# A feed-forward kernel on one core: each of the seven half-size products of the last block's first product formed from seven smaller ones

## The chip, the cores and the metric

One core of a Trainium2 chip. Times are device microseconds of one execution, from three runs of the kernel before; the profile is of one further execution. TensorE multiplies matrices into PSUM banks, VectorE (DVE in the profile) and ScalarE (ACT) read PSUM and SBUF, GpSimd (POOL) works on SBUF, and SyncE (SP) issues most of the DMAs.

## The reference

x is 64 batches of 64 rows of 512 features, all fp32. The conditioning part makes a row vector q per batch, mixes each row with the batch's sum, and multiplies by a 512 x 512 matrix; the second part multiplies by another 512 x 512 matrix and adds low-rank expert terms with a router:

```
q_emb = relu(cond @ W3 + b3)                      # one row of 512 for each batch
v     = (n * x + sum over rows of x) * q_emb      # 64 x 64 x 512
y     = relu(v @ W2 + b2)                         # the first wide product
gates = softmax(y @ W_router + b_router); the best 2 of 6 kept
out   = x + y @ W_base + b_base + (y @ A_s) @ B_s + sum over experts of ((y @ A_r) * gate) @ B_r
```

## The kernel before

Features lie on the 128 partitions, four chunks c of 128 features, and rows lie along the free dimension. The 4096 rows are worked in four blocks k of 1024; a block has two halves h of 512 rows. Every block does the same four stages on TensorE, one after the other: the first product (y from v and W2), the router and low-rank products (tile ph, line 573, 32 matmuls with y as the stationary operand), the second product (out from y and W_base), and in its midst the transposes of the gated low-rank values (tile pt) and their product with B.

Both wide products of a block are done in the seven-product form of a 2 x 2 block product. The weights are cut into b11 to b22 (256 x 256 each), the rows' features and halves into a11 to a22; weight_sums and row_sums make four sums of each (t and s, lines 133 and 241), VectorE does them with one instruction each. With P1 = a11 b11, P2 = a12 b21, P3 = s3 b22, P4 = a22 t3, P5 = s0 t0, P6 = s1 t1, P7 = s2 t2 the quarters of the result are P1 + P2, U + P5 + P3, U + P7 + P4 and U + P5 + P7, where U = P1 + P6. In the code a product is a call of product (line 147): two fp32 matmuls of 128 x 128 by 128 x 512 for one half j of a result quarter, so 14 calls and 28 matmuls for a block's first product.

first_seven (line 348) does the first product of blocks 1 to 3. For each j it opens four PSUM banks (px, py, pw, pz) of the six in pool ps_p, adds P2, P3 and P4 straight into the banks of P1, P5 and P7 (start=False), has VectorE add U and the banks in temporaries u, u22, u21, u12, and has ScalarE apply bias and relu into y. Pool tmp holds these temporaries, two buffers of 512 columns for each name; the second product uses the same names. first_mixed is block 0, where a half of the rows is done without the seven-product form and the other in it, with 256 columns a matmul.

While TensorE works on block k, the other engines get v and its row sums ready for block k + 1. prepare(k + 1) puts these steps into a list, behind: 17 steps of modulate (a sum on VectorE, 4 batches on ScalarE each) and the four row sums. fill(n) takes n of them and emits them at that place of the engines' queues: 6 for each j in first_seven, and in the second product nine times an equal share of what is left. A block's second product (second, line 417) opens eight results in the six banks, and its VectorE steps are: the gate (from ph), add_u, hw, add_r, and finish for each result, which adds the bias, and sends the result out through SyncE's queue. The tile pool's program order is the order of emission: each engine runs its queue in that order and waits for the others by semaphore.

x has three buffers for four blocks, v has two, and y, s and sy (the row sums of y) one each. ph is formed for half h and column group s in the order (0,0) (0,1) (1,0) (1,1) (0,2) (0,3) (1,2) (1,3), with c innermost.

Of the kernel before, what the change touches and what calls it, by code (L numbers as in the profile page):

```python
# [15 lines left out]
P = 128  # L16
# [18 lines left out]
def adaln_ffn(ctx: ExitStack, tc: tile.TileContext, xa, x0, x1, head, w3, w2, wb, a, bcat, br, outT):  # L35
# [11 lines left out]
    xpool = ctx.enter_context(tc.tile_pool(name="x", bufs=3))  # L47
    vpool = ctx.enter_context(tc.tile_pool(name="v", bufs=2))
    mid = ctx.enter_context(tc.tile_pool(name="mid", bufs=1))
    tmp = ctx.enter_context(tc.tile_pool(name="tmp", bufs=2))  # L50
    tmp1 = ctx.enter_context(tc.tile_pool(name="tmp1", bufs=1))
    small = ctx.enter_context(tc.tile_pool(name="small", bufs=1))
    ps_p = ctx.enter_context(tc.tile_pool(name="ps_p", bufs=6, space=PSUM))
# [80 lines left out]
    def weight_sums(w, name):  # L134

        b11, b12 = w[:, :KH, :DH], w[:, :KH, DH:]
        b21, b22 = w[:, KH:, :DH], w[:, KH:, DH:]
        t = [const.tile([P, KH, DH], F32, tag=f"{name}_{i}", name=f"{name}_{i}") for i in range(4)]
        steps = [
            lambda: nc.vector.tensor_tensor(t[0], b12, b11, ALU.subtract),  # L140
            lambda: nc.vector.tensor_tensor(t[1], b22, t[0], ALU.subtract),
            lambda: nc.vector.tensor_tensor(t[2], b22, b12, ALU.subtract),
            lambda: nc.vector.tensor_tensor(t[3], b21, t[1], ALU.subtract),
        ]
        return {1: b11, 2: b21, 3: b22, 4: t[3], 5: t[0], 6: t[1], 7: t[2]}, steps

    def product(ps, i, j, w, s, start=True):
        for c in range(KH):
# [92 lines left out]
    def row_sums(a, name, cols=slice(0, TB)):  # L241

        a11, a12, a21, a22 = a[:, :KH, 0, cols], a[:, KH:, 0, cols], a[:, :KH, 1, cols], a[:, KH:, 1, cols]
        s = [mid.tile([P, KH, TB], F32, tag=f"{name}{i}", name=f"{name}{i}")[:, :, cols] for i in range(4)]
        steps = [
            lambda: nc.vector.tensor_tensor(s[0], a21, a22, ALU.add),
            lambda: nc.vector.tensor_tensor(s[1], s[0], a11, ALU.subtract),
            lambda: nc.vector.tensor_tensor(s[2], a11, a21, ALU.subtract),
            lambda: nc.vector.tensor_tensor(s[3], a12, s[1], ALU.subtract),
        ]  # L250
        return {1: a11, 2: a12, 3: s[3], 4: a22, 5: s[0], 6: s[1], 7: s[2]}, steps

    behind = []

# [4 lines left out]
    def prepare(k):  # L259
        behind.extend(modulate(k))  # L260
        ss[k], steps = row_sums(vs[k], "s")
        behind.extend(steps)

    def relu(y, f, h, src, cols=slice(0, TB)):
        nc.scalar.activation(y[:, f, h, cols], src, AF.Relu, bias=b2_sb[:, f : f + 1])  # L265

    def first_mixed(y):

        vs[0] = v = vpool.tile([P, NC, 2, TB], F32, tag="v", name="v_0")
        vsum = small.tile([P, NC, BB], F32, tag="vsum", name="vsum_0")
        nq = small.tile([P, NC, BB], F32, tag="nq", name="nq_0")
        half, cols = BB // 2, BB // 2 * NH
        other = slice(cols, TB)
        s, s_steps = row_sums(v, "s", other)

        def part(p, c, f, lo, hi):
            nc.tensor.matmul(  # L279
                p[:, :, lo * NH : hi * NH], w2_sb[:, c, ts(f, P)], v[:, c, :, lo * NH : hi * NH],  # L280
                start=(c == 0 and lo == 0), stop=(c == NC - 1), skip_group_check=True,
            )

        def without_sums(c):
            for j in range(KH):
                nc.tensor.matmul(
                    px[j], w2_sb[:, c, ts(j, P)], v[:, c, 0, other], start=(c == 0), stop=(c % KH == KH - 1),
                    skip_group_check=True,
                )
            if c == KH - 1:  # L290
                for j in range(KH):
                    nc.scalar.copy(p1[j], px[j])

        idle(8)
        embed([0], "pq0")
        idle(2)
        p0 = [ps_p.tile([P, 2, cols], F32, tag="pp", name=f"py_{f}") for f in range(NC)]
        px = [ps_p.tile([P, cols], F32, tag="pp", name=f"yx_0_{j}") for j in range(KH)]
        p1 = [mid.tile([P, cols], F32, tag=f"p1_{j}", name=f"p1_0_{j}") for j in range(KH)]
        for c in range(NC):  # L300
            pieces = ((0, half // 2), (half // 2, half)) if c == 0 else ((0, half),)
            for lo, hi in pieces:
                modulate_group(v, vsum, c, lo, hi)
                for f in range(NC):
                    part(p0[f], c, f, lo, hi)
                if c == 0 and lo == 0:
                    embed(range(1, NC), "pq")
            if c > 0:
                modulate_scalar(v, vsum, nq, c - 1, half, BB)
            if c == NC - 1:  # L310
                modulate_scalar(v, vsum, nq, c, half, BB)
            if c > 1:
                without_sums(c - 2)
        for f in range(NC):
            nc.scalar.activation(y[:, f, :, :cols], p0[f], AF.Relu, bias=b2_sb[:, f : f + 1])
        for c in range(NC - 2, NC):
            without_sums(c)
        for step in t2_steps + s_steps:
            step()
        behind.extend(tb_steps)  # L320
        prepare(1)
        fill(1)
        for j in range(KH):
            relu(y, j, 0, px[j], other)
        for j in range(KH):
            f1, f2 = j, KH + j
            bank = lambda n: ps_p.tile([P, cols], F32, tag="pp", name=f"y{n}_0_{j}")
            temp = lambda n: tmp.tile([P, TB], F32, tag=n, name=f"{n}_0_{j}")[:, :cols]
            py, pw, pz = bank("y"), bank("w"), bank("z")
            u, r, r1, r2 = temp("u"), temp("u22"), temp("u21"), temp("u12")  # L330
            product(py, 6, j, t2, s)
            nc.vector.tensor_tensor(u, py, p1[j], ALU.add)
            product(pw, 5, j, t2, s)
            nc.vector.tensor_tensor(r, pw, u, ALU.add)
            product(pz, 7, j, t2, s)
            nc.vector.tensor_tensor(r, pz, r, ALU.add)
            relu(y, f2, 1, r, other)
            fill(1)
            product(pw, 3, j, t2, s, start=False)
            nc.vector.tensor_tensor(r2, pw, u, ALU.add)  # L340
            relu(y, f2, 0, r2, other)
            fill(1)
            product(pz, 4, j, t2, s, start=False)
            nc.vector.tensor_tensor(r1, pz, u, ALU.add)
            relu(y, f1, 1, r1, other)
            fill(1)

    def first_seven(k, y):

        s = ss[k]  # L350
        if k + 1 < NB:
            prepare(k + 1)
        for j in range(KH):
            f1, f2 = j, KH + j
            bank = lambda n: ps_p.tile([P, TB], F32, tag="pp", name=f"y{n}_{k}_{j}")
            temp = lambda n, pool=tmp: pool.tile([P, TB], F32, tag=n, name=f"{n}_{k}_{j}")
            px, py, pw, pz = bank("x"), bank("y"), bank("w"), bank("z")
            p1, u, r, r1, r2 = temp("p1", tmp1), temp("u"), temp("u22"), temp("u21"), temp("u12")
            product(px, 1, j, t2, s)
            nc.scalar.copy(p1, px)  # L360
            product(py, 6, j, t2, s)
            nc.vector.tensor_tensor(u, py, p1, ALU.add)
            fill(1)
            product(pw, 5, j, t2, s)
            nc.vector.tensor_tensor(r, pw, u, ALU.add)
            fill(1)
            product(pz, 7, j, t2, s)
            nc.vector.tensor_tensor(r, pz, r, ALU.add)  # L368
            relu(y, f2, 1, r)
            fill(2)  # L370
            product(px, 2, j, t2, s, start=False)
            relu(y, f1, 0, px)
            product(pw, 3, j, t2, s, start=False)
            nc.vector.tensor_tensor(r2, pw, u, ALU.add)
            relu(y, f2, 0, r2)
            fill(1)
            product(pz, 4, j, t2, s, start=False)
            nc.vector.tensor_tensor(r1, pz, u, ALU.add)
            relu(y, f1, 1, r1)
            fill(1)  # L380

    w = const.tile([P, 2 * NS, G], F32, tag="w", name="w")
    nc.gpsimd.memset(w[:, :, 0:1], 1.0)
# [33 lines left out]
    def second(k, y, ph):  # L417
# [6 lines left out]
                ps[name, j] = ps_p.tile([P, TB], F32, tag="pp", name=f"o{name}_{k}_{j}")  # L424
            product(ps[name, j], i, j, tb, sy, start=start)

        def temp(n, j, pool=tmp):
            return pool.tile([P, TB], F32, tag=n, name=f"o{n}_{k}_{j}")

        def copy_p1(j):  # L430
            p1s[j] = temp("p1", j, tmp1)
            nc.scalar.copy(p1s[j], ps["x", j])  # L432

        def add_u(j):
# [120 lines left out]
            last_routed(p, cols, hwd)  # L555
            leave(p, cols, 0, us12[1], queue)

    sys_ = {}
    t2, t2_steps = weight_sums(w2_sb, "t2")
    tb, tb_steps = weight_sums(wb_sb, "tb")  # L560
    for k in range(NB):
        y = mid.tile([P, NC, 2, TB], F32, tag="y", name=f"y_{k}")
        if k == 0:
            first_mixed(y)
        else:
            first_seven(k, y)


        ph = ps_h.tile([P, 2 * NS, P], F32, tag="ph", name=f"ph_{k}")

        for h, s in ((0, 0), (0, 1), (1, 0), (1, 1), (0, 2), (0, 3), (1, 2), (1, 3)):
            for c in range(NC):
                nc.tensor.matmul(  # L573
                    ph[:, h * NS + s, :HC], y[:, c, h, ts(s, P)], a_sb[:, c, :],
# [60 lines left out]
```

## Time and profile before

| | us |
|---|---|
| three runs: median (lowest to highest) | 267.84 (267.76 to 268.4) |
| the profiled execution: its time | 268.01 |
| its span, first to last instruction | 266.2 |
| last block: first product, by the chain of waits | 199.90 to 223.93 |
| last block: router products ph | 223.93 to 231.07 |
| last block: second product, to the last VectorE step | 231.07 to 263.3 |

The profile has a page of groups of instructions by line, engine and shape with their count, total and mean time; a chain of waits, followed back from the last instruction; and a timeline with, in brackets, how long an engine sat idle before an instruction and on whom it waited. An fp32 matmul appears as two MATMUL records and two weight loads (engine PEld). In the timeline a record's end is about 0.17 us behind the start of the next record, since matmuls are pipelined: four records of 512 columns are shown with 1.88 us and follow those before at a distance of 1.72. The chain gives the distances.

### The profile page before, as it was taken

The page shows a single profiled execution, that of the slowest core. Times are in us where ns is not written, and L with a number is a line of the kernel's source. Part 1 is how long each engine was busy: PE and PEld are TensorE (multiplying, and loading weights), DVE is VectorE, ACT ScalarE, POOL GpSimd, SP SyncE. Part 2 cuts the span into 40 slices and gives each one's busy share as a digit, 9 for nine tenths or more (in the row PEclk, how much of TensorE's full clock was granted, in tenths as well). Part 3 has the DMA queues.
Part 4 walks back from the last instruction along what each step waited for, and adds up shares of the span by engine and source line. Part 5 has one row for each costly group of instructions (what it writes and reads, how often), then busy time and mean ns, then how long its engine had stood idle before and what let it go on. Part 6 is the DMA issues. An engine that isn't in the chain of part 4 may idle for free.

```text
span 266.2 us, 2629 instructions
## 1 busy us (share of the span) xinstructions
PE 261.3 (98%) x878; PEld 141.6 (53%) x878; DVE 146.6 (55%) x251; ACT 112.8 (42%) x294; POOL 35.7 (13%) x41
## 2 busy tenths in 40 slices
PE   8999999999999999999999999999999999999995
PEld 4746895454444468454444448544444446845542
DVE  2896789646655448623746466823673333762422
ACT  2399389593028991254004996345000314001000
POOL 1000000570000000534000000057000000053400
PEclk9999999999999999999999999999999999999999
DMA  6999200004371000003230000000431000000323
GB/s 187 377 340 409 113 0 0 2 0 158 118 273 81 0 2 0 1 0 118 83 118 0 0 0 0 2 0 0 158 118 40 0 0 2 0 0 0 121 87 113
DMA packets 10303, 20.13 MB, mean 76 GB/s; under 512 B 1216, under 2 KB 3008, under 8 KB 10288
## 3 DMA queue, kind: packets, MB, share of 16 engines
q1 hardware_dynamic: 10000, 19.82, 20.7%
q10 hardware_dynamic: 288, 0.13, 0.2%
q8 instruction: 7, 0.11, 0.2%
q14 instruction: 8, 0.07, 0.1%
HBM read 11.56 MB, written 8.39 MB: 75 GB/s over the span
## 4 chain that ended last, share of the span: by engine, by line
PE 84%; ACT 7%; DVE 4%; DMA 2%; SPq 1%; issue 0%; DVEq 0%
PE oz L149 10%; PE ox L149 10%; PE ph L573 9%; PE ow L149 9%; PE yw L149 8%; PE yz L149 8%; PE yx L149 6%; PE oy L149 5%; PE ow L446 5%; PE yy L149 5%; ACT v L188 3%; PE ox L446 3%; PE oz L446 3%; DMA x<-in_x_dram 2%; ACT v L236 2%; ACT y L265 2%
## 5 line engine op out<-in xcount | busy, mean ns | idle before, releaser
L188 ACT ACTIVATE v<-x,vsum,nq 128x64 f32<-128x64 f32 x192 | 66.4, 429 | 6.7 <-DVE vsum L184 6.7
L440 POOL TENSOR_TENSOR ou<-ou,x 128x512 f32<-128x512 f32 x24 | 29.7, 1266 | 212.6 <-DVE ou L436 212.6
L573 PEld LDWEIGHTS ph<-a_sb,y 128*128 128x128 f32 x256 | 29.4, 192 | 2.2 <-issue 1.4
L573 PE MATMUL ph<-a_sb,y 128*128 128x118 f32 x256 | 29.7, 276 | 0.3 <-ACT y L265 0.3
L149 PE MATMUL ox<-y,wb_sb 128*128 128x512 f32 x64 | 29.5, 593 | 0.0
L265 ACT ACTIVATE y<-u,head_sb 128x512 f32<-128x512 f32 (+1 forms) x24 | 15.9, 664 | 25.0 <-DVE u L368 13.7
L149 PE MATMUL yx<-v,w_sb 128*128 128x512 f32 x48 | 22.6, 592 | 0.0
L360 ACT COPY p<-yx 128x512 f32<-128x512 f32 x6 | 3.5, 579 | 43.1 <-PE yx L149 43.1
L149 PEld LDWEIGHTS ox<-y,wb_sb 128*128 128x128 f32 x64 | 11.8, 190 | 12.9 <-issue 12.9
L452 DVE SCALAR_TENSOR_TENSOR ou<-ow,head_sb,ou 128x512 f32<-128x512 f32 x14 | 10.5, 751 | 11.9 <-PE ow L446 11.4
L436 DVE TENSOR_TENSOR ou<-oy,op 128x512 f32<-128x512 f32 x8 | 5.5, 687 | 17.9 <-PE oy L149 17.9
L149 PEld LDWEIGHTS yx<-v,w_sb 128*128 128x128 f32 x48 | 9.1, 190 | 11.5 <-issue 11.5
L149 PE MATMUL oz<-y,tb 128*128 128x512 f32 x32 | 15.1, 595 | 0.0
L149 PE MATMUL oz<-sy,tb 128*128 128x512 f32 x32 | 15.0, 592 | 0.0
L149 PE MATMUL oy<-sy,tb 128*128 128x512 f32 x32 | 15.0, 592 | 0.0
L279 PE MATMUL py<-v,w_sb 128*128 128x512 f32 (+1 forms) x40 | 14.4, 511 | 0.3 <-DVE v L228 0.3
L183 DVE TENSOR_REDUCE vsum<-x 128x16 f32<-128x1024 f32 x12 | 14.6, 1212 | 0.0
L432 ACT COPY op<-ox 128x512 f32<-128x512 f32 x8 | 4.7, 583 | 21.3 <-PE ox L149 21.3
L452 DVE SCALAR_TENSOR_TENSOR x<-ox,head_sb,x 128x512 f32<-128x512 f32 x8 | 6.0, 751 | 13.7 <-PE ox L446 13.7
L149 PE MATMUL yw<-s,w_sb 128*128 128x512 f32 (+1 forms) x32 | 13.4, 541 | 0.0
L149 PE MATMUL yy<-s,t 128*128 128x512 f32 (+1 forms) x32 | 13.3, 539 | 0.0
L149 PE MATMUL yw<-s,t 128*128 128x512 f32 (+1 forms) x32 | 13.3, 539 | 0.0
(109 smaller groups left out, 348.2 us busy)
## 6 DMA issues: line engine op xcount, KB each, us to landing
x<-in_x_dram SPq DMA_DIRECT2D x12, 512.0 KB, 7.3
out_dram<-ou SPq DMA_DIRECT2D x22, 256.0 KB, 2.0
out_dram<-x SPq DMA_DIRECT2D x8, 256.0 KB, 2.1
x<-in_x_dram SPq DMA_DIRECT2D x7, 256.0 KB, 5.7
w_sb<-in_w_dram SPq DMA_DIRECT2D x4, 256.0 KB, 5.6
wb_sb<-in_wb_dram SPq DMA_DIRECT2D x4, 256.0 KB, 4.9
w_sb<-in_w_dram SPq DMA_DIRECT2D x1, 384.0 KB, 4.6
out_dram<-ou SPq DMA_DIRECT2D x2, 192.0 KB, 1.9
```

Source lines behind the costliest of these rows:

```text
L149: nc.tensor.matmul(ps, w[i][:, c, ts(j, P)], s[i][:, c, :], start=start and c == 0, stop=c == KH - 1, skip_group_check=True,)
L183: nc.vector.tensor_reduce(vsum[:, c, :], xc, AX.XY, ALU.add)
L188: nc.scalar.activation(v[:, c, :, ts(b, NH)], xs[k][:, c, :, ts(b, NH)], AF.Identity, bias=vsum[:, c, b : b + 1], scale=nq[:, c, b : b + 1],)
L236: nc.scalar.activation(v[:, c, :, ts(b, NH)], batches_of(c, b, b + 1)[:, :, 0], AF.Identity, bias=vsum[:, c, b : b + 1], scale=nq[:, c, b ...
L265: nc.scalar.activation(y[:, f, h, cols], src, AF.Relu, bias=b2_sb[:, f : f + 1])
L279: nc.tensor.matmul(p[:, :, lo * NH : hi * NH], w2_sb[:, c, ts(f, P)], v[:, c, :, lo * NH : hi * NH], start=(c == 0 and lo == 0), stop=(c = ...
L432: nc.scalar.copy(p1s[j], ps["x", j])
L436: nc.vector.tensor_tensor(us[j], ps["y", j], p1s[j], ALU.add)
L440: nc.gpsimd.tensor_tensor(split(t[j], x.shape[1]), split(us[j], x.shape[1]), x, ALU.add)
L446: nc.tensor.matmul(ps[name, j], bcat_sb[:, ts(f, P)], hw, start=False, stop=True, skip_group_check=True)
L452: nc.vector.scalar_tensor_tensor(add, split(p, g), bb_sb[:, f : f + 1], add, ALU.add, ALU.add)
L573: nc.tensor.matmul(ph[:, h * NS + s, :HC], y[:, c, h, ts(s, P)], a_sb[:, c, :], start=(c == 0), stop=(c == NC - 1),)
```

## The change

In the last block (k = 3) the first product's seven products are each formed from seven smaller ones. A product of a (256 features x 512 rows) with b (256 x 256) is cut once more: 128 features, 256 rows and 128 outputs. One inner product q(n, t) is then one fp32 matmul of 128 x 128 by 128 x 256. All terms stay, in fp32.

- prepare_inner makes the inner sums. Weight side: four sums for each of the seven outer products, in 12 VectorE instructions (four on 4 x 128 columns, four on 2 x 128, four on 128), in a buffer of pool x; they are attached to steps 2 to 13 of the list behind, in block 2. Row side: four for outer product 1 (256 columns each), four for products 5, 6, 7 and 3 together (1024 columns), at the end of the list, and four for products 2 and 4 (512 columns), emitted in first_inner after the first four matmuls, in the buffer of sy. For this t and s become slices of one tile each.
- first_inner does the last block's first product. Each inner round t has two banks: a holds P1 and P5 in its left and right 256 columns, b holds U and U + P7. ScalarE copies P1 from a to the left of b (seed_y), where TensorE adds P6; it copies that to the right of b (seed_z), where TensorE adds P7 and later P4. P2 and P3 are added in a. VectorE takes the four quarters out with an add to what the outer form needs (ScalarE with a copy in the first two rounds, where there is nothing to add). The rounds overlap: round t's first two matmuls stand before the last ones of rounds t - 1 and t - 2. The outer sums U + P5 and U + P7 + P5 are four GpSimd adds, and the relus into y follow.
- The router products of the last block are formed in the order h = 0, then h = 1; rest(), with the last inner product q(4, 6), stands after the first two of eight groups.
- Pool tmp has one buffer of two times 512 columns for each name, and all users of these temporaries take the j-th half of a pair (temps).

```diff
-    tmp = ctx.enter_context(tc.tile_pool(name="tmp", bufs=2))
+    tmp = ctx.enter_context(tc.tile_pool(name="tmp", bufs=1))
...
-        t = [const.tile([P, KH, DH], F32, tag=f"{name}_{i}", name=f"{name}_{i}") for i in range(4)]
+        all_t = const.tile([P, 4, KH, DH], F32, tag=name, name=name)
+        t = [all_t[:, i] for i in range(4)]
...
-        s = [mid.tile([P, KH, TB], F32, tag=f"{name}{i}", name=f"{name}{i}")[:, :, cols] for i in range(4)]
+        all_s = mid.tile([P, 4, KH, TB], F32, tag=name, name=name)
+        s = [all_s[:, i, :, cols] for i in range(4)]
...
+    def temps(name):
+        return {n: tmp.tile([P, KH, TB], F32, tag=n, name=f"{n}_{name}") for n in ("u", "u22", "u21", "u12")}
...
+        if k == NB - 1:
+            prepare_inner(k)
+    def prepare_inner(k):
...
+        inner_t = t_flat[:, : 4 * 7 * P].rearrange("p (n o m) -> p n o m", n=4, o=7)
...
+        groups = ((slice(0, 4), lambda c, m: t2["sums"][:, :, c, ts(m, P)]),
+                  (slice(4, 6), lambda c, m: w_low[:, :, c, ts(m, P)]),
+                  (slice(6, 7), lambda c, m: t2[3][:, c, ts(m, P)].unsqueeze(1)))
+        t_steps = []
+        for o, b in groups:
+            t = [inner_t[:, n, o] for n in range(4)]
+            t_steps += [
+                lambda t=t, b=b: vectors(t[0], b(0, 1), b(0, 0), ALU.subtract),
+                lambda t=t, b=b: vectors(t[1], b(1, 1), t[0], ALU.subtract),
+                lambda t=t, b=b: vectors(t[2], b(1, 1), b(0, 1), ALU.subtract),
+                lambda t=t, b=b: vectors(t[3], b(1, 0), t[1], ALU.subtract),
+            ]
+        for n, step in enumerate(t_steps):
+            m, other = 2 + n, behind[2 + n]
+            behind[m] = lambda step=step, other=other: (other(), step())
...
+        sources = (("first", lambda c, r: vs[k][:, c, 0, ts(r, R2)].unsqueeze(1)),
+                   ("sums", lambda c, r: ss[k]["sums"][:, :, c, ts(r, R2)]),
+                   ("late", lambda c, r: vs[k][:, KH + c, :, ts(r, R2)]))
+        s_steps = [places]
+        for g, a in sources:
+            s_steps += [
+                lambda g=g, a=a: vectors(s[g][:, 0], a(0, 1), a(1, 1), ALU.add),
+                lambda g=g, a=a: vectors(s[g][:, 1], s[g][:, 0], a(0, 0), ALU.subtract),
+                lambda g=g, a=a: vectors(s[g][:, 2], a(0, 0), a(0, 1), ALU.subtract),
+                lambda g=g, a=a: vectors(s[g][:, 3], a(1, 0), s[g][:, 1], ALU.subtract),
+            ]
+        behind.extend(s_steps[:-4])
...
+        inner.update(t=t_of, s=s_of, e3=lambda: s["e3"], late=[late_places] + s_steps[-4:])
...
+    def first_inner(k, y):
...
+        order = (1, 5, 6, 7, 2, 3, 4)
+        late = inner["late"]
+        late.pop(0)()
+        pairs, e3 = temps(k), inner["e3"]()
+        p1, p5, u, v7 = (pairs[n] for n in ("u", "u22", "u21", "u12"))
+        plus = {1: None, 5: None, 6: p1, 7: u, 2: p1, 3: e3, 4: v7}
+        out = {1: p1, 5: p5, 6: u, 7: v7, 2: p1, 3: e3, 4: v7}
+        lo, hi = slice(0, TB // 2), slice(TB // 2, TB)
...
+        def open_banks(t):
+            for n in "ab":
+                bank[n, t] = ps_p.tile([P, TB], F32, tag="pp", name=f"i{n}_{t}")
+        def q(n, t):
+            o = order[t]
+            b, cols = {1: ("a", lo), 2: ("a", lo), 5: ("a", hi), 3: ("a", hi), 6: ("b", lo), 7: ("b", hi), 4: ("b", hi)}[n]
+            nc.tensor.matmul(
+                bank[b, t][:, cols], inner["t"](o, n), inner["s"](o, n), start=n == 1, stop=True,
+                skip_group_check=True,
+            )
+        def seed_y(t):
+            nc.scalar.copy(bank["b", t][:, lo], bank["a", t][:, lo])
+        def seed_z(t):
+            nc.scalar.copy(bank["b", t][:, hi], bank["b", t][:, lo])
+        def take_w5(t):
+            o = order[t]
+            r, w5 = out[o][:, 1, hi], bank["a", t][:, hi]
+            if plus[o] is None:
+                nc.scalar.copy(r, w5)
+            else:
+                add(r, w5, plus[o][:, 1, hi])
+        def take_u(t):
+            o = order[t]
+            c, y = out[o][:, 1, lo], bank["b", t][:, lo]
+            if plus[o] is None:
+                nc.scalar.copy(c, y)
+            else:
+                add(c, y, plus[o][:, 1, lo])
+        def take_22(t):
+            r = out[order[t]][:, 1, hi]
+            add(r, bank["b", t][:, hi], r)
+        def take_1(t):
+            o = order[t]
+            a, c, e = bank["a", t], out[o], plus[o]
+            if e is c:
+                add(c[:, :, lo], a.rearrange("p (j t) -> p j t", j=KH), c[:, :, lo])
+                return
+            if e is None:
+                nc.scalar.copy(c[:, 0, lo], a[:, lo])
+            else:
+                add(c[:, 0, lo], a[:, lo], e[:, 0, lo])
+            add(c[:, 1, lo], a[:, hi], c[:, 1, lo])
+        def take_21(t):
+            o = order[t]
+            c, z, e = out[o][:, 0, hi], bank["b", t][:, hi], plus[o]
+            if e is None:
+                nc.scalar.copy(c, z)
+            else:
+                add(c, z, e[:, 0, hi])
+        def relus(c, f, h, cols=slice(0, TB), js=range(KH)):
+            for j in js:
+                relu(y, f + j, h, c[:, j, cols], cols)
+        open_banks(0)
+        open_banks(1)
+        for t in range(2):
+            q(1, t)
+            q(5, t)
+            seed_y(t)
+            take_w5(t)
+        for step in late:
+            step()
+        q(2, 0)
+        q(6, 0)
+        take_u(0)
+        seed_z(0)
+        q(3, 0)
+        q(6, 1)
+        take_u(1)
+        seed_z(1)
+        q(7, 0)
+        take_22(0)
+        q(2, 1)
+        for t in range(2, 7):
+            open_banks(t)
+            take_1(t - 2)
+            q(1, t)
+            q(5, t)
+            seed_y(t)
+            q(4, t - 2)
+            take_21(t - 2)
+            q(7, t - 1)
+            take_22(t - 1)
+            if t > 2:
+                take_u(t - 1)
+            take_w5(t)
+            q(3, t - 1)
+            q(6, t)
+            seed_z(t)
+            if t > 2:
+                q(2, t - 1)
+            if order[t - 2] == 6:
+                for cols in (hi, lo):
+                    nc.gpsimd.tensor_tensor(e3[:, :, cols], u[:, :, cols], p5[:, :, cols], ALU.add)
+            if order[t - 2] == 7:
+                for cols in (lo, hi):
+                    nc.gpsimd.tensor_tensor(p5[:, :, cols], v7[:, :, cols], p5[:, :, cols], ALU.add)
+            if order[t - 2] == 2:
+                relus(p1, 0, 0)
+        take_1(5)
+        relus(e3, KH, 0, lo)
+        q(4, 5)
+        take_21(5)
+        relus(e3, KH, 0, hi)
+        q(7, 6)
+        take_22(6)
+        take_u(6)
+        relus(p5, KH, 1)
+        q(3, 6)
+        q(2, 6)
+        take_1(6)
+        relus(v7, 0, 1, lo)
+        def rest():
+            q(4, 6)
+            take_21(6)
+            relus(v7, 0, 1, hi)
+        return rest
...
+        elif k < NB - 1:
+            first_seven(k, y)
         else:
-            first_seven(k, y)
+            rest = first_inner(k, y)
...
-        for h, s in ((0, 0), (0, 1), (1, 0), (1, 1), (0, 2), (0, 3), (1, 2), (1, 3)):
+        inner_last = k == NB - 1
+        for n, (h, s) in enumerate(((0, 0), (0, 1), (0, 2), (0, 3), (1, 0), (1, 1), (1, 2), (1, 3)) if inner_last
+                     else ((0, 0), (0, 1), (1, 0), (1, 1), (0, 2), (0, 3), (1, 2), (1, 3))):
+            if inner_last and n == 2:
+                rest()
```

In the left-out lines t_of and s_of give for each outer product o and inner n the slice that holds its operand (a quarter of the weights or rows themselves for some n, an inner sum for the others), places and late_places allocate the buffers of the row sums, and first_mixed, first_seven and second take their temporaries from pairs.

## The prediction

> **What bounds the kernel now.** I read the page's first part, then the chain of waits, then busy time by stage.
>
> ```profile
> PE 261.3 (98%) x878; PEld 141.6 (53%) x878; DVE 146.6 (55%) x251; ACT 112.8 (42%) x294; POOL 35.7 (13%) x41
> ```
> ```profile
> 199.90 1.72 PE yx L149 x4
> ...
> 222.22 1.72 PE yz L149 x4
> 223.93 7.14 PE ph L573 x64
> 231.07 1.73 PE ox L149 x4
> ```
> ```profile
> core 0: us, PE busy (x) PEld busy (x) DVE busy (x) ACT busy (x) POOL busy (x), PEclk, DMA share, GB/s
> 199.90:223.90 24.00, 24.00 (x58) 10.60 (x58) 6.97 (x10) 6.15 (x9) 0.00 (x0) 1.00 0.03 12
> ```
>
> TensorE is busy 98% and the chain of the last block is PE pieces only, each beginning where the last ended. So TensorE time saved here moves the end one for one, and each hole in its stream is lost. The third view is the stage that is rewritten: PE full at clock 1.00, VectorE busy 7 of 24 us, ScalarE 6. The other engines have room; the question is whether they answer in time.
>
> **What TensorE saves.** Durations come from rows kept apart by shape:
>
> ```profile
> L149 PE MATMUL yz<-s,t 128*128 128x512 f32 x24 | 11.3, 592 | 0.0
> L149 PE MATMUL yz<-s,t 128*128 128x256 f32 x8 | 2.1, 379 | 0.0
> L292 ACT COPY p<-yx 128x256 f32<-128x256 f32 x2 | 0.6, 359 | 0.0
> L334 DVE TENSOR_TENSOR u<-yw,u 128x256 f32<-128x256 f32 x2 | 0.8, 425 | 0.5 <-PE yw L149 0.4
> ```
>
> An fp32 matmul leaves two records. Four records of 512 columns take 1.72 us in the chain, so a matmul takes 0.86; four of 256 columns take 0.86 (next fence), so 0.43, exactly half. The stage has 14 products of 2 matmuls: 28 x 0.86 = 24.05 us. After: 7 outer products of 7 matmuls of 256 columns: 49 x 0.43 = 21.05. **Saved: 3.0 us, if TensorE is never kept waiting.** A load of weights of 0.19 us fits under each 0.215 us record already in those 256-column rows.
>
> **What a crossing costs.** The inner form passes partial sums between engines inside a bank. The trace shows one such pass with nothing to cover it:
>
> ```profile
> 31.25 0.86 PE yz L149 x4
> 32.11 0.93 PE yw L149 x4
> ```
> ```profile
> 31.43 0.42 DVE L334 TENSOR_TENSOR u<-yw,u 128x256 f32<-128x256 f32 x1
> 31.91 0.73 PEld L149 LDWEIGHTS yw<-s,w_sb 128*128 128x128 f32 x4 [0.20 <-DVE u L334]
> ```
>
> VectorE reads bank yw until 31.85; the weight load of the next product into it starts at 31.91, and the four records take 0.07 more than elsewhere, so the matmul's slot moved from 31.95 to 32.02: 0.17 us from a reader's end to TensorE's slot. The other way: four yz records start at 26.77, their slots end 0.86 later at 27.63, VectorE starts on them at 27.83: 0.20. Neighbouring VectorE adds of 256 columns start 0.34 apart (28.77, 29.11), ScalarE instructions about 0.10 sooner than their durations.
>
> **A rule against this change.** The Trainium skill, "PSUM — Partial Sum Buffer", section "PSUM bank collisions raise a hardware error", says no two of TensorE, VectorE and ScalarE may be in one bank and partition quadrant at once, two reads included. The change puts four quarter results into two banks, so users of different halves must take turns. The trace agrees that waits are coarser than the data: the first copy out of pt needs four transposes, the eight start from 244.6 to 245.4, and it starts at 245.8, after all of them. I walked the new stage with waits by bank: holes of 1.04 us; by halves, 0.77. I take 1.04.
>
> **The walk, from the first inner matmul as zero** (q(n,t): inner product n of the t-th outer one; outer order 1, 5, 6, 7, 2, 3, 4).
> - Head. q(1,0) and q(5,0) end their slots at 0.86, ScalarE sees them at 1.06, seed_y takes 0.36, take_w5 (started 0.26 later) ends at 1.68. q(2,0) writes that bank: 1.68 + 0.17 = 1.85. q(1,1) and q(5,1) cover only to 1.72: **0.14 lost.** q(6,0) is seen at 2.92; ScalarE copies u (to 3.28), then seed_z (3.31 to 3.67); q(7,0) can go at 3.84, but q(3,0) and q(6,1) end at 3.57: **0.27 lost.**
> - Middle. A round is 7 x 0.43 = 3.01 us of TensorE against 6 VectorE adds at 0.34 (2.05) and 2 ScalarE copies at 0.26. The tightest cover, seed_y before q(6,t), has 0.55 us to spare. Nothing lost. Without that cover each of five rounds would lose the shortfall.
> - Tail. seed_z(6) ends at 19.44; behind it in ScalarE's queue stand relu p1 twice (717 ns in the row of 512-column relus, 0.62 apart), then e3's low half twice (508 ns, 0.41 apart), ending at 21.49. The first router matmul reads e3 and goes at 21.66; q(2,6) ended at 21.02: **0.64 lost.** rest() then covers v7: its last relu ends at 25.46, its first reader is due at 27.44.
>
> Sum: -3.01 + 0.14 + 0.27 + 0.64 = **-1.95 us** from the start of the stage to the first ox.
>
> **What is added elsewhere, and its cover.**
> - *Twelve weight sums* (four each of 512, 256 and 128 columns: rows of 690, 425 and 288 ns, each about 0.08 less from start to start, 4.6 us) on VectorE, ten in block 2's first product, where it is busy 12.35 of 24.10 us. Put into its queue there they delay one add (L365, by 0.17) and one sum by 0.3, and neither has a waiter that soon. The slot of x they need is free about 131.6 (block 1's x result leaves PE at 128.75, add 0.75, landing 2.1); the first is due at 144.7. Cost 0. That stage is held by ScalarE (0.3 us before ph), which gains no work.
> - *Eight row sums* in block 2's second product, two steps a share for one. These land behind TensorE's results:
>
> ```profile
> 197.36 0.75 DVE L452 SCALAR_TENSOR_TENSOR ou<-ow,head_sb,ou 128x512 f32<-128x512 f32 x1 [0.63 <-PE ow L446]
> 198.02 1.22 DVE L249 TENSOR_TENSOR s<-v,s 128x1024 f32<-128x1024 f32 x1
> 200.00 0.75 DVE L452 SCALAR_TENSOR_TENSOR ou<-ow,head_sb,ou 128x512 f32<-128x512 f32 x1 [0.76 <-PE ow L446]
> ```
>
>   Two 1.22 us steps ahead of each L452 push the first to 197.9 and the second to 200.85. Waiting behind the second: its output DMA, the bank (first wanted about 5 us into the stage), and the four late sums (0.69 each), which run from +1.8 to +4.4. The first add TensorE depends on, take_22(0), is due at +4.5. Cost 0, with 0.4 us to spare.
> - *One pair buffer for two singles.* The same bytes. The last user of u12 lands about 202.8 (200.75 + 2.0); v7 is first written at +9.9, about 209.6. Cost 0.
> - *POOL's four adds* (1.27 each): e3's two end at +13.5 and +14.8, its first reader comes at +15.9; p5's end at +17.4, their relus start at +22.2. Cost 0.
> - *Relus later than router order.* The four y sums begin at 25.5 and end at 30.2; the router ends at 29.2, so the gate starts 0.66 late on VectorE. The first to feel it:
>
> ```profile
> 237.22 0.69 DVE L443 TENSOR_TENSOR ou<-oz,ou 128x512 f32<-128x512 f32 x1 [0.38 <-POOL ou L440]
> 239.50 1.88 PE L149 MATMUL oz<-y,tb 128*128 128x512 f32 x4
> ```
>
>   It ends at 237.91, plus 0.17; TensorE comes at 239.50: 1.4 us of room for 0.66. Cost 0.
>
> **A price not in the trace:** a ScalarE copy from PSUM into PSUM. The nearest row, PSUM to SBUF, says 359 ns. The skill's "ScalarE: Activation LUTs", section "What ACT_TABLE_LOAD costs", gives 186 + 0.833 ns per column, 399 here, and calls writes to PSUM faster ("Step-by-step"). Estimated with 0.40 the stage gains 1.74 us; with 0.28, 2.3. I take the row; both stay in the range.
>
> **Time.** The profiled execution took 268.01 us (span 266.2 and 1.8 around it); less 1.95 it would be 266.06. The median shown, 267.84, is 0.17 lower: **265.9 us.**
>
> **Rivals.**
> 1. *The holes close* (relus a little shorter, copies into PSUM quicker): up to the full 3.0, so 264.8 to 265.3. For: ScalarE idles in the middle. Against: the relu queue at the tail is five instructions deep. 0.13.
> 2. *Dearer crossings.* Instructions that wait for two engines may cost more than the single waits I priced: +0.1 us per crossing leaves 1.34, +0.2 leaves 0.74, +0.25 leaves 0.43. For: no row has PE, ACT and DVE taking turns in one bank. Against: where the trace shows a wait it is 0.17 to 0.20. 267.1 to 267.4; 0.17.
> 3. *Slower: VectorE's backlog at the seam.* If it reaches the late sums over 2.3 us after the first inner matmul, take_22(0), and with it q(4,0) and all behind it, moves one for one; from 4.1 us the gain is gone, at 5 us the time is 268.7. For: 24 added VectorE steps, strided views without a row. Against: rows of one size agree within 1% whatever their operands (1214 to 1226 ns). 0.08.
>
> My own case: 0.62, with 265.3 to 266.5 as its own range. About 0.3%, 0.8 us, can be told from no change here. All of my case and rival 1 lie beyond it, and about half of rival 2: faster 0.83, same 0.09, slower 0.08. The range, 264.8 to 267.3, runs from no holes to crossings dearer by 0.2.
>
> **What would show it.** About 42 more PE records (98 of 256 columns for 56 of 512); the piece from the first inner matmul to the first ox 29.2 us, not 31.17; PE idle near 0.4 at the head behind ScalarE and 0.6 before the router behind L265 (or its new line). I am wrong if PE idles in each round, if q(4,0) waits for VectorE, or if a block before the last changes.

## The result, and the profile after

The median went from 268.11 us (267.76 to 268.4, four executions) to **265.44 us** (265.05 to 265.59, four executions). The ratio is 0.9899, with a 95% interval from 0.988 to 0.9917. The forecast was 265.9 in a range from 264.8 to 267.3, with faster at 0.83. The time lies in the range, 0.46 below the forecast.

The profiled execution after took 265.05 us, span 263.3. From the first part of its page, the busy time of each engine, its share of the span and its instructions:

```profile
PE 257.9 (98%) x920; PEld 148.8 (57%) x920; DVE 168.4 (64%) x296; ACT 119.2 (45%) x318; POOL 43.8 (17%) x45
```

TensorE has 920 records where it had 878: the 42 more that were forecast. It is still busy 98% of the span, now of a shorter one. VectorE, ScalarE and GpSimd all work more, and the span is shorter all the same.

The chain of waits of the same profile, through the stage that was rewritten (start, length, what):

```profile
199.53 2.30 PE ia L480 x10
201.83 0.43 PE ib L480 x2
202.27 0.43 PE ia L480 x2
202.70 1.00 PE ib L480 x4
203.70 1.29 PE ia L480 x6
...
219.67 0.86 PE ia L480 x4
220.54 1.78 PE ph L801 x16
222.31 0.44 PE ib L480 x2
222.75 5.35 PE ph L801 x48
228.10 1.73 PE ox L150 x4
```

From the first inner matmul to the first ox it is 228.10 - 199.53 = 28.57 us, where the chain of before gave 231.07 - 199.90 = 31.17: **2.60 less**, and 1.95 was forecast. From the first ox to the end the two kernels agree (35.13 before, 35.20 after). The holes are read off the records: ten of them should take 10 x 0.215 = 2.15 us and the first piece has 2.30, so 0.15 is lost; the four ib records of 1.00 us lose 0.14. In front of ph, at 220.54, there is no hole.

The two profiles differ by 2.96 us in all. The other 0.37 of that is there already at 23 us, before any of the work that was rewritten, and isn't counted for the change: among kernels that are the same up to the last block, the profiles below reach that block anywhere between 199.53 and 201.77. The stage's length in the chain doesn't depend on that, so the experiments are read by it first. Medians of one kernel differ by 0.3 us between series.

The view of busy time by stage, for the stretch from the first inner matmul to the router:

```profile
core 0: us, PE busy (x) PEld busy (x) DVE busy (x) ACT busy (x) POOL busy (x), PEclk, DMA share, GB/s
199.53:220.54 21.01, 21.01 (x99) 18.08 (x98) 15.70 (x35) 9.27 (x26) 5.00 (x4) 1.00 0.06 20
```

VectorE went from 7 of 24 us to 15.7 of 21, the clock stayed at 1.00. The weight loads now fill 18 of 21 us, still below the matmuls.

### The profile page after: what moved, and what is told of

Its sections match the earlier page's. It is cut to its first block, busy times and chain, and to the rows that moved or that the text cites. A ratio compares the mean times of both kernels' runs of the same rounds, so it can differ in the third digit from the quotient of the medians.

```text
span 263.3 us, 2789 instructions
## 1 busy us (share of the span) xinstructions
PE 257.9 (98%) x920; PEld 148.8 (57%) x920; DVE 168.4 (64%) x296; ACT 119.2 (45%) x318; POOL 43.8 (17%) x45
## 4 chain that ended last, share of the span: by engine, by line
PE 91%; ACT 5%; DMA 2%; DVE 1%; SPq 0%; issue 0%; DVEq 0%
PE oz L150 11%; PE ox L150 10%; PE ph L801 10%; PE ow L150 9%; PE py L354 5%; PE yw L150 5%; PE yz L150 5%; PE oy L150 5%; PE ia L480 5%; PE ow L668 5%; PE yx L150 4%; PE ib L480 4%; PE yy L150 3%; ACT v L189 3%; PE ox L668 3%; PE oz L668 3%
## 5 line engine op out<-in xcount | busy, mean ns | idle before, releaser
L189 ACT ACTIVATE v<-x,vsum,nq 128x64 f32<-128x64 f32 x192 | 66.3, 429 | 6.7 <-DVE vsum L185 6.7
L662 POOL TENSOR_TENSOR u_o<-u_o,x 128x512 f32<-128x512 f32 x24 | 31.9, 1356 | 178.3 <-DVE u_o L658 178.3
L674 DVE SCALAR_TENSOR_TENSOR u_o<-ow,head_sb,u_o 128x512 f32<-128x512 f32 x14 | 10.5, 748 | 8.5 <-PE ow L668 8.2
L658 DVE TENSOR_TENSOR u_o<-oy,op 128x512 f32<-128x512 f32 x8 | 5.5, 688 | 15.5 <-PE oy L150 15.5
L150 PE MATMUL yx<-v,w_sb 128*128 128x512 f32 x32 | 15.0, 592 | 0.0
L437 ACT COPY p<-yx 128x512 f32<-128x512 f32 x4 | 2.3, 576 | 27.7 <-PE yx L150 27.7
L150 PE MATMUL ow<-sy,tb 128*128 128x512 f32 x28 | 13.2, 593 | 0.0
L150 PE MATMUL ow<-sy,wb_sb 128*128 128x512 f32 x28 | 13.2, 592 | 0.0
L486 ACT COPY ib<-ia 128x256 f32<-128x256 f32 x7 | 2.5, 357 | 21.2 <-PE ia L480 21.2
L237 ACT ACTIVATE v<-x,vsum,nq 128x64 f32<-128x64 f32 x32 | 10.9, 427 | 1.7 <-DVE vsum L235 1.7
```

Source lines behind the costliest of these rows:

```text
L150: nc.tensor.matmul(ps, w[i][:, c, ts(j, P)], s[i][:, c, :], start=start and c == 0, stop=c == KH - 1, skip_group_check=True,)
L189: nc.scalar.activation(v[:, c, :, ts(b, NH)], xs[k][:, c, :, ts(b, NH)], AF.Identity, bias=vsum[:, c, b : b + 1], scale=nq[:, c, b : b + 1],)
L237: nc.scalar.activation(v[:, c, :, ts(b, NH)], batches_of(c, b, b + 1)[:, :, 0], AF.Identity, bias=vsum[:, c, b : b + 1], scale=nq[:, c, b ...
L658: nc.vector.tensor_tensor(us[j], ps["y", j], p1s[j], ALU.add)
L662: nc.gpsimd.tensor_tensor(split(t[j], x.shape[1]), split(us[j], x.shape[1]), x, ALU.add)
L674: nc.vector.scalar_tensor_tensor(add, split(p, g), bb_sb[:, f : f + 1], add, ALU.add, ALU.add)
```

## The experiments

All times are set against the kernel before on the same chip, as a ratio with its 95% interval. "Stage" is the chain's length from the first inner matmul to the first ox.

### The change once more

This is the changed kernel as it is, beside the next three, so that they have a measure from the same chip.

> The changed kernel once more, as the yardstick of this set: 265.4 us, 0.990 of the kernel before. Start of the stage to the first ox 28.6 us, two holes of about 0.15 us in TensorE's stream at the head, none in front of the router products.

265.72 us, ratio 0.9913 (0.9881 to 0.9945); stage 28.57. The stage comes out the same to the hundredth, while the median differs by 0.28 from the one above.

### Where did the hole before the router go?

The forecast lost 0.64 us there: the first router matmul was to wait for all four feature chunks of y. The trace of after shows TensorE and ScalarE side by side (the timeline; brackets give how long the engine was idle and on whom it waited):

```profile
218.41 0.36 ACT L489 COPY ib<-ib 128x256 f32<-128x256 f32 x1 [1.37 <-PE ib L480]
218.68 1.33 ACT L340 ACTIVATE y<-u,head_sb 128x512 f32<-128x512 f32 x2
219.92 1.69 ACT L340 ACTIVATE y<-inner_late,head_sb 128x256 f32<-128x256 f32 x4
220.37 1.94 PE L801 MATMUL ph<-a_sb,y 128*128 128x118 f32 x16
```

The second of the four relus on e3 (inner_late), with a line of its own:

```profile
220.32 0.49 ACT L340 ACTIVATE y<-inner_late,head_sb 128x256 f32<-128x256 f32 x1
```

TensorE starts on ph at 220.37, while ScalarE is still at the second of these four: they are chunks 2 and 3. ScalarE's queue is as long as forecast, but c is the innermost loop of the router: the first group begins with chunks 0 and 1, which are the two relus of 218.68, and reads chunk 3 six records later, at 220.37 + 6 x 0.111 = 221.04 (16 records take 1.78 in the chain). The relu that it needs ends at 220.81, and with the crossing of 0.17 that is 220.98. So by this sum the wait is there, covered by 0.06 us.

**Chunks in reverse.** If that is so, the same work with the chunks of the first group in the order 3, 2, 1, 0 has to lose the 0.6 us:

```diff
+            chunks = list(range(NC))
+            if inner_last and n == 0:
+                chunks.reverse()
-            for c in range(NC):
+            for c in chunks:
...
-                    start=(c == 0), stop=(c == NC - 1),
+                    start=(c == chunks[0]), stop=(c == chunks[-1]),
```

> Only the first router group of the last block takes its four chunks of y in reverse order. Theory (waits are by chunk, and the order of the chunks covers the relus): the chunk that ScalarE finishes last is now read first; its relu ends at 220.81 by the trace of the changed kernel, TensorE is there at 220.37, so a hole of 0.6 us opens and the time goes to about 266.0. Rival (the hole I forecast is missing because the relus themselves are earlier than I walked them): no hole in either order, time unchanged at 265.4.

The ratio is 0.9919 (0.989 to 0.9949), median 266.15; the stage takes 29.17, **0.60 more**. The chain of waits now leaves TensorE:

```profile
219.35 1.15 ACT y L340 x2
220.50 0.90 ACT y L340 x2
221.41 0.04 issue
221.45 2.04 PE ph L804 x16
```

TensorE stands behind ScalarE's second relu on e3, just as the forecast had it. What was wrong in the forecast was which chunk the router reads first. The medians (266.15 against 265.72) can't tell the two kernels apart; the stage can.

**The old order of groups.** The change also puts rest() two groups into the router and does the upper half of the rows last. Here rest() comes before the router, and the groups run as before:

```diff
-        inner_last = k == NB - 1
-        for n, (h, s) in enumerate(((0, 0), (0, 1), (0, 2), (0, 3), (1, 0), (1, 1), (1, 2), (1, 3)) if inner_last
-                     else ((0, 0), (0, 1), (1, 0), (1, 1), (0, 2), (0, 3), (1, 2), (1, 3))):
-            if inner_last and n == 2:
-                rest()
+        if k == NB - 1:
+            rest()
+        for h, s in ((0, 0), (0, 1), (1, 0), (1, 1), (0, 2), (0, 3), (1, 2), (1, 3)):
```

> The last inner product and its relus stand before all router products, and these have the order of the other blocks. Theory (the new order is there to cover v7's relus): the third group reads v7's left half, whose relu ends at 223.2 while TensorE comes at 222.6; with the second chunk a hole of 0.8 to 1.0 us, time about 266.3. Rival (the order is worth nothing, ScalarE is early enough): 265.4.

266.65 us, ratio 0.9941 (0.9921 to 0.9961); the stage takes 29.55, 0.98 more. Its chain of waits, and its timeline around rest()'s q(4, 6), the ib records:

```profile
220.71 3.32 ACT y L340 x7
224.03 0.04 issue
224.07 5.79 PE ph L799 x48
```
```profile
220.73 0.59 PE L480 MATMUL ia<-v,t 128*128 128x256 f32 x2
221.37 0.30 PEld L480 LDWEIGHTS ib<-v,inner_t 128*128 128x128 f32 x2 [0.45 <-DVE u L471]
221.37 0.70 PE L480 MATMUL ib<-v,inner_t 128*128 128x256 f32 x2
```

In the old order the third group reads the upper half of the rows, and TensorE waits until 224.07 for the relus of that half, and once more for the next chunk. Part of the 0.98 is lost earlier, and the forecast of this run had left it out: with no router products in front of it, q(4, 6) waits for VectorE, which still reads its bank. It could have gone at 221.16 (0.43 behind 220.73) and goes at 221.48 (its records are shown 0.11 longer than elsewhere): 0.32 of the 0.98, which leaves 0.66 for the relus. With both put back the stage gains 1.62 us in place of 2.60: over a third of the gain hangs on the order of the router's groups and on the place of rest(). The run moves both at once; the split is read from its trace alone.

### The two holes at the head

The forecast had 0.14 and 0.27; the chain shows 0.15 and 0.14. The weight loads and ScalarE in the timeline of after:

```profile
201.13 0.30 PEld L480 LDWEIGHTS ia<-v,w_sb 128*128 128x128 f32 x2 [0.28 <-ACT u L495]
...
202.30 0.37 ACT L503 COPY u<-ib 128x256 f32<-128x256 f32 x1 [0.36 <-PE ib L480]
...
202.57 0.38 ACT L489 COPY ib<-ib 128x256 f32<-128x256 f32 x1
203.00 0.30 PEld L480 LDWEIGHTS ib<-inner_s,inner_t 128*128 128x128 f32 x2 [0.28 <-ACT ib L489]
```

Both stand where they were put: behind take_w5(0) (L495) for q(2,0), and behind seed_z(0) (L489) for q(7,0). But seed_z started 0.27 after take_u (L503), where the walk had started it at take_u's end, 0.39 after: on the one engine that does both, the second does not wait for the first to end. That is most of the 0.13 by which the hole is smaller.

**Three rounds at the head.** If TensorE has nothing else to do there, a third round ahead of q(2,0) should fill both:

```diff
         open_banks(0)
         open_banks(1)
+        open_banks(2)
-        for t in range(2):
+        for t in range(3):
             q(1, t)
             q(5, t)
             seed_y(t)
-            take_w5(t)
+            if t < 2:
+                take_w5(t)
         for step in late:
             step()
+        take_w5(2)
         q(2, 0)
         q(6, 0)
...
         seed_z(1)
+        q(2, 1)
         q(7, 0)
         take_22(0)
-        q(2, 1)
-        for t in range(2, 7):
+        take_1(0)
+        q(3, 1)
+        q(6, 2)
+        seed_z(2)
+        q(7, 1)
+        take_22(1)
+        q(4, 0)
+        take_21(0)
+        for t in range(3, 7):
```

> Three rounds instead of two are opened at the head, so that TensorE has 0.86 us more of work before it needs ScalarE's first two answers. Theory (the two head holes are ScalarE's answer time and can be covered): both close, the stage takes 28.3 us, time about 265.1, 0.3 us less than the changed kernel. Rival (the holes come from the waits themselves, so they move elsewhere, or VectorE at the seam takes their place): 265.4 or more.

The stage takes 28.29, 0.28 less, and neither hole is left. The median is 265.61, ratio 0.9913 (0.9882 to 0.9945), not to be told from the change. Since take_w5(2) stands ahead of take_22(0) here, a quarter of u gets p1's quarter without the last term that take_22(0) adds: this kernel leaves that term out of y. The next kernel sets the add behind:

```diff
         for step in late:
             step()
-        take_w5(2)
         q(2, 0)
...
         take_22(0)
+        take_w5(2)
         take_1(0)
```

> Three rounds opened at the head as in e5_head, but the add that takes round 2's W5 stands behind the one that completes round 0's quarter, on which it builds (in e5_head it stood ahead of it, so there that quarter of y lacked the round's last term). Theory: the same stage as e5_head, 28.3 us from the first inner matmul to the first ox against 28.57 for the changed kernel, no hole at the head; time about 265.1 to 265.3. Rival (the new place of that add holds VectorE or TensorE): a hole in front of q(3,2) or q(4,0), 28.5 or more.

**265.17 us** (264.98 to 265.5), ratio 0.9889 (0.9871 to 0.9907), the lowest of all that compute every term. Stage 28.30. The head in its chain of waits:

```profile
199.84 3.02 PE ia L480 x14
202.87 0.43 PE ib L480 x2
```

Fourteen records in 3.02 us are 0.216 each, with no hole in it, and the pieces behind it have none. The 0.27 us of the stage are seen in the chain; the medians alone wouldn't show them, and the changed kernel did not run beside this one on its chip.

### Is there slack at the seam?

Rival 3 was a VectorE that comes late to the inner sums, so that take_22(0) and all of TensorE behind it move. Here the four late sums are done twice, to the same values:

```diff
-        for step in late:
+        for step in late + late:
```

> The four late row sums are done twice over on VectorE (the same values are written again), 2.4 us more of its time at the seam. Theory of rival 3 (VectorE's backlog decides beyond a slack): in the trace of the changed kernel take_22(0) starts at 203.74 and TensorE needs it by 205.26, 0.17 after its end, so 0.93 us of the 2.4 are free and 1.5 us are lost, in front of q(4,0): 266.9. Had I been right with 0.4 us of room, 2.0 lost: 267.4. Rival (VectorE at the seam is not on the path): 265.4.

267.69 us, ratio 0.9987 (0.9971 to 1.0002): the gain is nearly gone. The stage takes 30.50, 1.93 more. The timeline of this kernel behind the doubled sums:

```profile
206.90 0.41 DVE L471 TENSOR_TENSOR u<-ib,u 128x256 f32<-128x256 f32 x1
...
207.37 0.70 PE L480 MATMUL ib<-v,inner_t 128*128 128x256 f32 x2 [1.66 <-DVE u L471]
```

And the same two instructions, take_22(0) and q(4,0), in the timeline of after:

```profile
203.74 0.42 DVE L471 TENSOR_TENSOR u<-ib,u 128x256 f32<-128x256 f32 x1
...
204.83 0.59 PE L480 MATMUL ib<-v,inner_t 128*128 128x256 f32 x2
```

TensorE now waits for VectorE in front of q(4,0). take_22(0) starts 6.66 us after the first inner matmul (which the chain has at 200.24); in the change it starts 4.21 after (203.74 against 199.53). It moved by 2.45 and the end by 1.93, so 0.5 us of slack lay ahead of it. That is what the forecast said (0.4), and not the larger slack that I had read from the trace of after before this run: I had taken the wrong matmul for q(4,0). It is the one at 204.83, and 204.83 - (204.16 + 0.17) is again 0.50. So rival 3's mechanism is real, and beyond the slack its price is one for one: 2.45 less 0.50 is 1.95, and 1.93 were lost. In the change VectorE is simply in time.

### What costs nothing

**The pair buffers alone**, in the kernel before:

```diff
-    tmp = ctx.enter_context(tc.tile_pool(name="tmp", bufs=2))
+    tmp = ctx.enter_context(tc.tile_pool(name="tmp", bufs=1))
...
+    def temps(name):
+        return {n: tmp.tile([P, KH, TB], F32, tag=n, name=f"{n}_{name}") for n in ("u", "u22", "u21", "u12")}
...
```

The left-out lines let every user of the temporaries take its half of a pair.

> The kernel before, with only the temporaries changed to one pair buffer for two single ones. Both theories of mine say no change: within 0.3% of the kernel before. If a pair's later release holds an engine back, blocks 1 to 3 each show a new wait in front of the first use of u12, and the time rises.

268.21 against 268.23 us, ratio 0.9998 (0.9984 to 1.0011). No difference, as costed; the stage takes 31.17 as before (231.27 - 200.10).

**Sums moved out of GpSimd's way.** In the trace of after, some of VectorE's row sums in block 2 take up to twice as long as the same sums elsewhere (the last section has the lines). Here the weight sums are packed into block 2's first product, and the shares of its second product are set so that no sum of two SBUF operands runs while GpSimd adds:

```diff
-            m, other = 2 + n, behind[2 + n]
+            m = 2 + n * 10 // 12
+            other = behind[m]
...
+        planned = [2, 2, 1, 0, 3, 3, 3, 2, 2] if k == NB - 2 else None
...
-            fill(-(-len(behind) // left[0]))
+            fill(planned[9 - left[0]] if planned else -(-len(behind) // left[0]))
```

> The changed kernel with the list's steps of block 2 handed out differently: all twelve weight sums within the first product, and no sum whose two operands lie in SBUF beside GpSimd's adds. Theory (VectorE and GpSimd slow each other down only when both read two operands from SBUF at once, and idle VectorE time hides it): the three row sums go back from 2.0, 1.7 and 2.3 us to 1.22, GpSimd's adds beside them from about 1.9 to 1.27, and the time stays at 265.4 within 0.3, since the seam is 1 us later on VectorE and has 0.9 of room. Rival (the slow sums have another cause, such as their position after ScalarE's writes): they stay slow.

265.39 us, ratio 0.9896 (0.9884 to 0.9909), stage 28.58. The three row sums take 1.21 to 1.23 us again, and the time is no shorter: nothing that TensorE needed had waited for them.

### Is TensorE alone the bound of the middle?

Three inner matmuls are left out here, q(2, t) for t = 2, 3 and 4; the waits on the other engines stay.

```diff
-            if t > 2:
+            if t > 5:
                 q(2, t - 1)
```

> Leaves out three of the 49 inner matmuls (q(2,t) for t of 2, 3 and 4), so these terms are missing in y. Theory (TensorE alone bounds the middle of the stage, at 0.43 us a matmul): 1.3 us less than the changed kernel, 264.1. Rival (the rounds are already held by VectorE or the crossings, so that TensorE's time is not the price): less than 0.6 us gained.

264.33 us, ratio 0.9855 (0.9842 to 0.9868); the stage takes 27.28, 1.29 less, which is 3 x 0.43. The first line is from the chain of after, where a round has six ia records in one piece; the second is the same place in this kernel:

```profile
209.31 1.29 PE ia L480 x6
```
```profile
209.93 0.86 PE ia L480 x4
```

Every matmul that goes shortens the stage by its whole length, even with a round of 2.58 us in place of 3.01. So down to rounds of that length no other engine bounds the middle, and the matmuls saved are worth their full length.

## Why the prediction was right, and where it was off

- **What TensorE saves: right.** -3.01 from 28 matmuls of 0.86 to 49 of 0.43. Three fewer give 1.29, so the price per matmul is 0.43 in place. With the two holes added back the stage gained 2.89; about 0.1 us of the 3.01 is missing, since the inner records follow each other by 0.216 and not by 0.215 (78 records from 203.70 to 220.54).
- **First head hole: right**, 0.15 for 0.14. The crossings of 0.17 and 0.20, taken from the one uncovered pass of before, hold inside one bank with three engines too. That speaks against rival 2 (dearer crossings): at +0.1 us each the walk lost 0.6 more than forecast, and the stage lost less than forecast.
- **Second head hole: mis-sized**, 0.14 for 0.27. The step that failed: "ScalarE copies u (to 3.28), then seed_z (3.31 to 3.67)" lets a copy wait for the end of the one before it on the same engine, although the prediction had itself noted that ScalarE instructions start about 0.10 us sooner than their durations.
- **Middle: right**, nothing lost; five rounds without a hole.
- **Tail: mis-sized**, 0 for 0.64. The step that failed is "The first router matmul reads e3 and goes at 21.66". It is the fifth that reads e3's chunk 2 and the seventh that reads chunk 3, counted in records; the first reads p1's. ScalarE's queue itself was walked rightly. The reversed order shows that the hole of 0.60 is there as soon as the router asks in the other order. Nothing in the prediction foresaw the cover, and it is 0.06 us thin: that this term came out at nothing was luck.
- **Waits by bank rather than by half: right for what is seen.** seed_y(0) reads the half that q(1,0) wrote, finished at 199.97, and starts after q(5,0) in the other half has ended. And at 207.44 VectorE waits for a ScalarE copy that only reads the other half of the bank. The temporary that both write is not the reason: at 203.74 (the line under the seam above) VectorE and ScalarE write two quarters of one temporary at the same moment, out of different banks. The timeline of after:

```profile
199.37 0.60 PE L480 MATMUL ia<-v,w_sb 128*128 128x256 f32 x2
199.80 0.59 PE L480 MATMUL ia<-inner_s,inner_t 128*128 128x256 f32 x2
200.43 0.36 ACT L486 COPY ib<-ia 128x256 f32<-128x256 f32 x1 [16.93 <-PE ia L480]
...
203.74 0.38 ACT L518 COPY u<-ia 128x256 f32<-128x256 f32 x1
...
207.03 0.38 ACT L518 COPY u<-ia 128x256 f32<-128x256 f32 x1
207.44 0.42 DVE L471 TENSOR_TENSOR u<-ia,u 128x256 f32<-128x256 f32 x1 [0.79 <-ACT u L518]
```

- **PSUM to PSUM by ScalarE: the row was near.** 0.36 us was taken from the nearest row; the copy takes 357 ns on average (seven L486), and the same shape from PSUM to SBUF 373 to 378 in this stage. The prediction's 399 was too long for both: the Trainium skill's sum in "ScalarE: Activation LUTs", section "What ACT_TABLE_LOAD costs", is for an ACTIVATE, and the trace lists these as COPY. That a copy into PSUM is the quicker one agrees, by 10 to 20 ns (L489, into PSUM too, takes 363).
- **The seam: right**, 0.5 us of slack for 0.4, shown by the doubled sums.
- **The costs set at nothing: right in the time, not all in the detail.** The sums beside GpSimd's adds took longer than their rows, which the prediction hadn't seen coming; the cover was long enough. The gate was to start 0.66 late, a slip in the sum: its own figures, 30.2 less 29.2, give 1.0. It starts 1.04 after the ph of the chain ends, where it was 0.04 before (231.11 against 231.07). Its first reader still has room, by the timeline of after:

```profile
229.14 0.20 DVE L609 TENSOR_TENSOR lg<-ph,br_sb 128x48 f32<-128x48 f32 x1
...
235.31 0.69 DVE L665 TENSOR_TENSOR u_o<-oz,u_o 128x512 f32<-128x512 f32 x1 [0.45 <-POOL u_o L662]
...
236.53 1.02 PE L150 MATMUL oz<-y,tb 128*128 128x512 f32 x2
```

  L665 ends at 236.00, with the crossing 236.17, and TensorE comes at 236.53: 0.36 us are left of the 1.4.
- **The time.** The stage gained 0.65 more than forecast (0.64 at the tail, 0.13 at the head, less about 0.1 for the records' distance). The median of before, in the new series, is 0.27 higher than the one shown then. 265.9 - 0.65 + 0.27 is 265.5; 265.44 was measured. The result lies in the forecast's own range (265.3 to 266.5), near its end towards rival 1. That the tail hole would close was rival 1's case, but not for its reason, shorter relus: they are as long as forecast.

## What to carry to other kernels

When a product waits on a producer, ask for each instruction which part of the operand it reads, and in which order: the innermost loop of the reader can hide a queue that the sum puts on the path, and reversing it is a cheap experiment that shows whether it does. Splitting a product once more gave 2.60 of the 3.01 us here, since TensorE was the only bound; the holes came only where the rounds start, and one more round opened at the start closed them. Read the gain from the stage in the chain of waits, where hundredths repeat, before the median, where tenths don't.

## What the runs showed that was not expected

VectorE and GpSimd take turns where both read SBUF. The timeline of after in block 2's second product, with a line for each GpSimd add:

```profile
180.62 1.27 POOL L662 TENSOR_TENSOR u_o<-u_o,x 128x512 f32<-128x512 f32 x1 [4.22 <-DVE u_o L658]
180.95 2.02 DVE L248 TENSOR_TENSOR s<-v 128x1024 f32<-128x1024 f32 x1 [0.41 <-ACT v L189]
181.85 2.26 POOL L662 TENSOR_TENSOR u_o<-u_o,x 128x512 f32<-128x512 f32 x1
182.90 0.68 DVE L665 TENSOR_TENSOR u_o<-oz,u_o 128x512 f32<-128x512 f32 x1
183.50 1.69 DVE L249 TENSOR_TENSOR s<-s,v 128x1024 f32<-128x1024 f32 x1
184.07 2.24 POOL L662 TENSOR_TENSOR u_o<-u_o,x 128x512 f32<-128x512 f32 x1
185.11 2.28 DVE L250 TENSOR_TENSOR s<-v 128x1024 f32<-128x1024 f32 x1
186.27 2.25 POOL L734 TENSOR_TENSOR hwd<-hwT 112x512 f32<-112x512 f32 x1
```

And the same work in the kernel with the sums moved away:

```profile
180.83 3.72 POOL L663 TENSOR_TENSOR u_o<-u_o,x 128x512 f32<-128x512 f32 x3 [4.34 <-DVE u_o L659]
...
187.54 1.21 DVE L248 TENSOR_TENSOR s<-v 128x1024 f32<-128x1024 f32 x1
```

Alone, the sum of 1024 columns takes 1.21 us and a GpSimd add 1.27; beside each other they take 1.69 to 2.28. The ends tell why. VectorE's three sums and GpSimd's four adds end in turn at 181.89, 182.97, 184.11, 185.19, 186.31, 187.39 and 188.52, each 1.08 to 1.14 after the one before. So one stands still until the other has ended, although both are shown as under way. VectorE's add at 182.90, with one operand in PSUM, keeps its 0.68 beside GpSimd. The Trainium skill, "SBUF — State Buffer", section "Who interferes with whom", names just this pair, a VectorE instruction with two SBUF inputs against a GpSimd instruction that reads SBUF, and calls the shared ports an exclusive lock; these ends agree. None of it reached the end here, as the run with the sums moved shows, but a sum on the path would pay for it: 1.07 us for the one at 185.11.

The other number worth keeping is that ScalarE's copies follow each other by 0.27 us at a duration of 0.38: for a walk of an engine's queue the distance of the starts is the price, and the duration counts only for whoever waits at the end.
